# Keys and queries of rotary attention's first pair, made in the last period of the eight-bit pipeline

## The chip, the cores and the metric

The kernel runs on one core of one Trainium2 chip. The metric is the device time of one execution in microseconds (us), and the time of a kernel is the median over its runs. The engines are TensorE (PE; its weight loads are listed as PEld), VectorE (DVE), ScalarE (ACT), GpSimd (POOL) and SyncE (SP, which issues the DMAs). Each works through its own queue of instructions in order and waits on semaphores for the others.

## The reference, cut to what matters

The reference is a stack of four gated layers, each an attention-like block and a feed-forward block on `x` of shape 32 x 64 x 256 in float32, with a second input `ctx_2048` of the same shape:

```python
x = x + tanh(g_xattn[2]) * _L2_xattn_ref(_layernorm(x), ctx, mask, ...)   # block 4
x = x + tanh(g_ffn[2])   * _L2_ffn_ref(_layernorm(x), ...)                # block 5
x = x + tanh(g_xattn[3]) * _L3_xattn_ref(_layernorm(x), ctx, ...)         # block 6
x = x + tanh(g_ffn[3])   * _L3_ffn_ref(_layernorm(x), ...)                # block 7
```

Block 4 is cross attention whose query and output projections round their input and weights to eight bits, with one scale per row (`round(x / s)`, where `s = max|x| / 127`). Block 5 is a gated feed-forward network, `bit_linear(silu(bit_linear(x)) * bit_linear(x))`, which rounds each input in the same way and uses ternary weights. Block 6 is attention with rotary positions. There the 64 rows of a sequence are channels (8 heads of 8) and the 256 columns are positions:

```python
q = _apply_rotary(q_emb, split_heads(_proj(x, Wq, bq)))
k = _apply_rotary(k_emb, split_heads(_proj(c, Wk, bk)))
v = split_heads(_proj(c, Wv, bv))
scores = einsum('bhtc,bhsc->bhts', q, k) / sqrt(8)
out = einsum('bhts,bhsc->bhtc', softmax(scores), v)
```

## The kernel before

`x` stays in SBUF as 16 tiles (`NT`) of 128 rows by 256 columns. Since a sequence has 64 rows, a tile is two sequences, a pair. Blocks run one after another, and neighbours overlap.

**Blocks 4 and 5** run together in `blocks45`, a software pipeline that is written out by hand. `PERIOD` (L930) is a list of small operations, each with the number of tiles that it lags behind:

```python
xn:0 pk:0 hq5:5 r5:3 exp:2 t50:3 pv51:4 v50:4 gbo:0 vb50:4 qT:1 pat1:2 pat0:2 am:0 s50:3 pg51:4 sx:0 v51:4 aT1:2 g51:4
```

This is its first line. In period n an operation `name:back` works on tile n - back. Lags 0 to 2 belong to block 4 and lags 2 to 5 to block 5 (names with a 5). The periods run from n = 0 to 20. In period 17 block 4 works on its last tile and in period 18 its pools are closed. Every engine runs its instructions in just the order in which these operations emit them: the whole part is under a manual schedule.

The operations that the steps below name, by engine and by their lines in the profile:

- DVE: `xn` (layer norm of the next tile, L167), `xn5` (the same for block 5, L167 too), `hq5`, `xq`, `xq5` and `oq` (scaled for rounding, all L1003), `e0` and `e1` (scores plus mask, L1146), `g50` and `g51` (gate halves, L1349), `y` (L1260), `bn5` and `ag5` (statistics of block 5, L1272 and L1277), `am5h` (largest hidden value of each row, shown with all such maxima as L987).
- POOL: `sub` (scores minus their maximum, L1172), `xy` (x plus y, L1264), `gob5` (L1305), `gbo` (L1045), `vb50` and `vb51` (value half plus bias, L1358), `gv51` and `gv50` (gate half times value half, L1362).
- ACT: `exp` (L1176), `v50` and `v51` (L1354), `silu5` (L1380, with a table load before it).
- PE: products of the projections, among them `pg5` and `pv5` (L1343), and transposes (L1009).
- `w0` and `w1` (DVE and POOL): one part each of layer-norm statistics for a coming group of four tiles (`stats`, L1023). A group has eight parts: a `bn_stats` and `bn_aggr` for each tile (L110, L113), then `ln_nv` on POOL (L124) with a first guess of the inverse root on DVE (L92), then three Newton steps of four POOL operations each (L100 to L103). The last group that block 4 needs is made in periods 1 to 4. From period 5 on `w0` and `w1` emit nothing.

Block 4 uses, among others, the PSUM bank `pc` (pool `pm4`), the score tiles `e` and the tile `aT` in pool `t4`, and the places `wk` (its key weights) and `mask` in the tile `wb` of its weights.

**Block 6** (`block6`, L1445) begins with period 18. Its first `next` sets up: `gbo`, three `clear` rounds of memsets for `mx` and `va` on POOL, the statistics of tiles 0 to 3 with `_stats` on DVE (L110 to L124, L92 to L98), and `start(0)`. `start(i)` makes keys, values and queries of pair i. It takes `xn` (L167), eight products for the keys from `ctx` and eight for the queries from `xn` (L1506), the values (L1520), two rotations of two operations each on DVE (L1513), and on POOL the sum for the keys `k` (L1528), their two copies `kb` masked by head parity (L1531) and the sum for the queries `q` (L1534). Then come 140 steps g, each with score products `pp` (L1573) and the DVE reduction to `mx` (L1579), and six steps later the shifted scores `pw` (L1563) and their exponential (L1565). While periods 18 to 20 of block 5 are still being emitted, one step g is emitted at every sixth operation.

`ctx` in the layout that block 6 reads is loaded over the old one by SP at the start of period 17.

Of the kernel before, what the change touches and what calls it, by code (L numbers as in the profile page):

```python
# [17 lines left out]
F32 = mybir.dt.float32  # L18
# [4 lines left out]
ALU = mybir.AluOpType  # L23
# [3 lines left out]
P = 128  # L27
# [100 lines left out]
def _stats(c, pool, i0=0, n=NT, bufs=1, here=False):  # L128

    mv = pool.tile([P, max(n, 4), 2], F32, tag="ln_mv", name="ln_mv", bufs=bufs)[:, :n]  # L130
    for j in range(n):
        _mean(c, pool, mv[:, j, :], i0 + j, here)
    return mv, _inverse(c, pool, mv, "ln", bufs), i0


def _stats_slowly(c, pool, i0, n, bufs, on=None):

    mv = pool.tile([P, n, 2], F32, tag="ln_mv", name="ln_mv", bufs=bufs)
    for j in range(n):
        _mean(c, pool, mv[:, j, :], i0 + j)  # L140
        yield None
    yield from (None if r is None else (mv, r, i0) for r in _inverse_slowly(c, pool, mv, "ln", bufs, on))
# [20 lines left out]
def _norm(c, pool, ln, i, bufs=4):  # L163
    mv, rs, i0 = ln
    j = i - i0
    xn = pool.tile([P, D], F32, tag="xn", name="xn", bufs=bufs)
    c.nc.vector.tensor_scalar(xn, c.x[:, i, :], mv[:, j, 0:1], rs[:, j : j + 1], ALU.subtract, ALU.mult)  # L167
    return xn
# [770 lines left out]
def blocks45(c, kw):  # L939
# [26 lines left out]
    with ExitStack() as es:  # L966
# [53 lines left out]

        def stats(a):  # L1023
            if not more and a.i and len(lns) < NT // 4:
                more.append(_stats_slowly(c, sm4, 4 * len(lns), 4, 2, nc.gpsimd))
            if more and (ln := next(more[0])):
                lns.append(ln)
                more.clear()
# [326 lines left out]

        def biased(a, n):
            cols = slice(n * 512, (n + 1) * 512)
            nc.gpsimd.tensor_tensor(a.v[:, cols], a.v[:, cols], vb[:, cols], ALU.add)  # L1358

        def times(a, n):  # L1360
            cols = slice(n * 512, (n + 1) * 512)
            nc.gpsimd.tensor_tensor(a.g[:, cols], a.g[:, cols], a.v[:, cols], ALU.mult)  # L1362

        def hturned(a, n):
            a.ph[n] = turned(ps5, "ps", "ph", a.hq, 4, 4 * n)
# [44 lines left out]
        def x5(a):  # L1410
            _add_gated(c, a.i, a.po5, a.co)

        period = [(name, int(back)) for name, back in (t.split(":") for t in PERIOD.split())]
        last4 = max(back for name, back in period if name not in fifth)
        tiles = [SimpleNamespace(i=i, pat=None) for i in range(NT)]
# [14 lines left out]
        gwo = sm5.tile([P, 1], F32, tag="gwo", name="gwo")  # L1430
        nc.vector.tensor_scalar(gob, ob, c.gate[:, 6:7], None, ALU.mult)
        nc.vector.tensor_tensor(gwo, gw[:, 2:3], c.gate[:, 6:7], ALU.mult)
        for n in range(NT + max(back for _, back in period)):
            if n == NT + last4:
                es4.close()
            for name, back in period:
                if 0 <= n - back < NT and (back or n):
                    ops[name](tiles[n - back])
                    yield n - NT, n >= NT + last4

# [4 lines left out]
def block6(c):  # L1445
# [17 lines left out]
    with ExitStack() as es:  # L1463
# [16 lines left out]
        nc.vector.tensor_tensor(gbo, pb, _v(c.l3x, L3X, "bo"), ALU.add)  # L1480
        nc.vector.tensor_tensor(gbo, gbo, c.gate[:, 3:4], ALU.mult)
        mxs, vas = [], []
        for n in range(3):
            if n < 2:
                mx = sm.tile([P, 2, 4, 32], F32, tag=f"mx{n}", name=f"mx{n}")
                nc.gpsimd.memset(mx.rearrange("p t j r -> p (t j r)"), 0.0)
                mxs.append(mx)
            va = sm.tile([P, 2, 2, HN, 32], F32, tag=f"va{n}", name=f"va{n}")
            nc.gpsimd.memset(va.rearrange("p n k h r -> p (n k h r)"), 0.0)
            nc.gpsimd.memset(va.rearrange("p n k h r -> p (n k h) r")[:, :, HC], 1.0)  # L1490
            vas.append(va)

        def start(i):


            xn = _norm(c, tp, lns[i // 4], i, bufs=2)
            ctx = c.ctx.rearrange("p k t -> p (k t)")[:, i * D : (i + 1) * D]
            yield

            def project(w, src):  # L1500

                pp = pair("pp")
                for r in range(2):
                    for m in range(2):
                        rows = slice(m * S, (m + 1) * S)
                        nc.tensor.matmul(pp[:, m, r, :], w[rows, r, :], src[rows, :], start=True, stop=True)  # L1506
                return pp

            def rotate(pp, n):

                t = [tp.tile([P, 2, D], F32, tag=f"t{r}", name=f"t{r}") for r in range(2)]
                for r, f in enumerate((cos, sin)):
                    nc.vector.scalar_tensor_tensor(t[r], pp[:, :, r, :], bias[:, n, r : r + 1], f, ALU.add, ALU.mult)  # L1513
                return t

            a = [SimpleNamespace(i=i, n=n, e={}, mx=mxs[n]) for n in range(2)]
            pk = project(wk, ctx)
            pv = pair("pv").rearrange("p a b d -> p (a b d)")[:, : 2 * P].rearrange("p (j o) -> p j o", j=2)
            for j in range(2):
                nc.tensor.matmul(pv[:, j, :], ctx[:, j * P : (j + 1) * P], wv, start=True, stop=True)  # L1520
            pq = project(wq, xn)
            va = vas[i % 3]
            for n in range(2):
                src = pv[:, :, n * S : (n + 1) * S].rearrange("p k (h d) -> p k h d", d=HC)
                nc.scalar.copy(va[:, n, :, :, :HC], src)
            t = rotate(pk, 1)
            k = tp.tile([P, 2, D], F32, tag="k", name="k", bufs=1)
            nc.gpsimd.tensor_tensor(k, t[0], t[1], ALU.add)  # L1528
            kb = tp.tile([P, 2, 2, D], F32, tag="kb", name="kb", bufs=3)
            for h in range(2):  # L1530
                nc.gpsimd.tensor_scalar(kb[:, :, h, :], k, odd[:, h : h + 1], None, ALU.mult)  # L1531
            t = rotate(pq, 0)
            q = tp.tile([P, 2, D], F32, tag="q", name="q", bufs=3)
            nc.gpsimd.tensor_tensor(q, t[0], t[1], ALU.add)  # L1534
            o = tp.tile([P, 2, 2, S], F32, tag="o", name="o")
            for n in range(2):
                a[n].q, a[n].k, a[n].v, a[n].o = q[:, n], kb[:, n], va[:, n], o
            yield a
# [4 lines left out]
        def shift(a):  # L1543

            pt = ps1.tile([P, D], F32, tag="a", name="pt")
            for t in range(2):
                nc.tensor.transpose(pt[:, t * P : (t + 1) * P], a.mx[:, t].rearrange("p j r -> p (j r)"), c.ident)
            yield
            a.qs = tp.tile([P, D], F32, tag="qs", name="qs")
            nc.vector.tensor_tensor(a.qs, pt, a.q, ALU.add)  # L1550

        def scores(w, p, g, parts):
# [23 lines left out]
            for part in parts:  # L1576
                next(part, None)
            if p:
                nc.vector.tensor_reduce(p.mx[:, t, i0 : i0 + 2, 16:18], pp, AX.X, ALU.max, negate=True)  # L1579

        def mix(a, h):

# [35 lines left out]

        lns, more = [_stats(c, sm, 0, 4, bufs=2)], None
        seqs = list(start(0))[-1]
        yield
        steps, ahead = [[] for _ in range(4 * B + 13)], [[] for _ in range(4 * B + 13)]

# [375 lines left out]
```

## Time and profile before

| | |
|---|---|
| runs | 1333.27, 1330.69, 1333.59 us; median 1333.27 |
| profiled execution | 1334.85 us, of which the span is 1333.1 |
| mean granted TensorE clock | 0.97 |
| PE, DVE, ACT, POOL busy | 90%, 68%, 46%, 34% of the span |
| period of blocks 4 and 5 (starts of `sub`) | 605.53, 616.79, 629.30, 645.12, 657.64, 670.16 |
| first `mx` of block 6 | 812.93 |

In the lines of a timeline, the columns are the start in us after the span's start, the duration in us (of all that are joined under an xN), the engine, the line of the kernel, the operation, its output and inputs, and the shape. The bracket at the end is how long the engine stood idle before it, with what ended that wait. PEclk is the clock that PE was granted, in tenths of full speed in the page and as a fraction in the windows. A line of a window gives the stretch and its length, then for PE, PEld, DVE, ACT and POOL the busy us with the number of instructions, then the clock and the DMA's share and rate.

### The profile page before, as it was taken

How to read it: one execution, taken by the hardware profiler on the slowest of the kernel's cores; microseconds unless marked ns; L12 is line 12 of the kernel's file. 1: busy time of each engine (PE TensorE's matmuls, PEld its weight loads, DVE VectorE, ACT ScalarE, POOL GpSimd, SP SyncE). 2: the span in 40 equal slices, each digit the busy share in tenths (PEclk: the TensorE clock that was granted, in tenths of full speed). 3: DMA queues.
4: the chain of work that ended last, by engine and by line, in shares of the span. 5: the costliest groups of instructions: out<-in, count | busy, mean ns of one | idle time of the engine just before them, and what ended most of it. 6: DMA issues, size and time to landing. Idle time of an engine off the chain costs nothing.

```text
span 1333.1 us, 21452 instructions
## 1 busy us (share of the span) xinstructions
PE 1199.2 (90%) x8342; PEld 724.3 (54%) x8342; DVE 905.1 (68%) x2195; ACT 618.0 (46%) x1046; POOL 456.1 (34%) x479
## 2 busy tenths in 40 slices
PE   0788899999999989988899976899999999999999
PEld 0666345454533367765666642455555555555665
DVE  6588867554348898768999996587787877532111
ACT  2553634322231145657899971455555555511100
POOL 3333606120123233335777775123225335000000
PEclk9899999989999999989999997799999999999999
DMA  6000000100052120000000010100000000000000
GB/s 216 21 1 16 0 0 1 63 1 0 8 213 97 33 103 1 1 0 2 2 2 2 2 64 1 60 37 1 2 2 1 2 2 1 1 8 8 16 16 16
DMA packets 10294, 34.14 MB, mean 26 GB/s; under 512 B 1360, under 2 KB 5968, under 8 KB 8528
## 3 DMA queue, kind: packets, MB, share of 16 engines
q1 hardware_dynamic: 10192, 32.76, 6.9%
q8 instruction: 66, 1.08, 0.4%
q14 instruction: 36, 0.29, 0.1%
HBM read 30.66 MB, written 2.10 MB: 25 GB/s over the span
## 4 chain that ended last, share of the span: by engine, by line
PE 56%; DVE 28%; POOL 5%; ACT 4%; issue 4%; DMA 2%; SPq 0%; DVEq 0%; POOLq 0%; ACTq 0%
PE pw L1563 6%; PE po L1586 5%; PE pp L1573 4%; PE po L1735 4%; PE pu L1725 4%; PE pg L1725 4%; PE pc L610 3%; PE pu L462 2%; PE pg L462 2%; PE pu L465 2%; PE pa L509 2%; PE po L515 2%; PE pg L465 2%; DVE xn L167 2%; DMA w<-in_l2f 1%
## 5 line engine op out<-in xcount | busy, mean ns | idle before, releaser
L1579 DVE TENSOR_REDUCE mx<-pp 128x4 f32<-128x1024 f32 x128 | 155.9, 1218 | 42.3 <-PE pp L1573 41.8
L1565 ACT ACTIVATE e<-pw 128x1024 f32<-128x1024 f32 x128 | 130.9, 1025 | 115.0 <-PE pw L1563 68.5
L1563 PE MATMUL pw<-qs,kb 32*128 32x256 f32 x1024 | 147.1, 408 | 7.5 <-DVE qs L1550 4.5
L1573 PE MATMUL pp<-kb,q 32*128 32x512 f32 x512 | 148.8, 665 | 4.8 <-POOL q L1534 4.0
L1563 PEld LDWEIGHTS pw<-qs,kb 32*128 32x128 f32 x1024 | 88.5, 187 | 52.3 <-issue 29.4
L468 ACT ACTIVATE sg<-pg 128x512 f32<-128x512 f32 (+1 forms) x75 | 37.8, 512 | 117.1 <-PE pg L462 51.6
L610 PE MATMUL pc<-xw,wb 64*64 64x512 f32 x768 | 90.0, 600 | 0.2 <-DVE x L542 0.2
L1728 DVE TENSOR_TENSOR h<-pu,sg 128x512 f32<-128x512 f32 x32 | 22.1, 692 | 80.8 <-PE pu L1725 80.8
L1727 ACT ACTIVATE sg<-pg 128x512 f32<-128x512 f32 x32 | 19.1, 597 | 122.8 <-PE pg L1725 122.7
L469 DVE TENSOR_TENSOR h<-pu,sg 128x512 f32<-128x512 f32 (+1 forms) x75 | 42.5, 573 | 49.1 <-PE pu L462 30.4
L1528 POOL TENSOR_TENSOR k<-t,t 128x512 f32<-128x512 f32 x16 | 20.3, 1268 | 148.4 <-DVE t L1513 148.4
L1586 PE MATMUL po<-e,va 128*32 128x256 f32 x1024 | 69.0, 387 | 1.8 <-ACT e L1565 1.8
L768 POOL TENSOR_TENSOR acc<-acc,sq 128x512 f32<-128x512 f32 x28 | 39.0, 1392 | 65.1 <-ACT sq L767 63.6
L1725 PE MATMUL pg<-xf,wa 128*128 128x512 f32 x128 | 60.3, 592 | 0.0
L1725 PE MATMUL pu<-xf,wa 128*128 128x512 f32 x128 | 60.3, 592 | 0.0
L610 PEld LDWEIGHTS pc<-xw,wb 64*64 64x64 f32 x768 | 29.9, 134 | 53.9 <-issue 53.2
L1735 PE MATMUL po<-hb,h 128*128 128x256 f32 x256 | 55.9, 379 | 0.0
L1735 PEld LDWEIGHTS po<-hb,h 128*128 128x128 f32 x256 | 48.6, 190 | 8.3 <-issue 1.9
L110 DVE BATCH_NORM_STATS2 ln_st<-x 128x6 f32<-128x256 f32 x112 | 44.1, 408 | 10.9 <-POOL x L1615 7.2
L1586 PEld LDWEIGHTS po<-e,va 128*32 128x32 f32 x1024 | 26.9, 109 | 44.3 <-issue 17.5
L1513 DVE SCALAR_TENSOR_TENSOR t<-pp,wb,con 128x512 f32<-128x512 f32 x64 | 45.0, 745 | 8.7 <-PE pp L1506 8.7
L1531 POOL TENSOR_SCALAR kb<-k,con 128x512 f32<-128x512 f32 x32 | 49.8, 1569 | 1.6
(342 smaller groups left out, 2946.8 us busy)
## 6 DMA issues: line engine op xcount, KB each, us to landing
w<-in_l2f SPq DMA_DIRECT2D x12, 512.0 KB, 3.9
wa<-in_l0f SPq DMA_DIRECT2D x2, 1828.0 KB, 13.0
wa<-in_l1f SPq DMA_DIRECT2D x2, 1536.0 KB, 9.4
wa<-in_l3f SPq DMA_DIRECT2D x2, 1536.0 KB, 8.0
wb<-in_conv SPq DMA_DIRECT2D x1, 2048.0 KB, 7.4
ctx<-in_ctxT SPq DMA_DIRECT2D x2, 1024.0 KB, 6.0
ctx<-in_ctxN SPq DMA_DIRECT2D x2, 1024.0 KB, 6.3
out<-x SPq DMA_DIRECT2D x16, 128.0 KB, 1.7
```

The lines of the kernel that those rows point to most:

```text
L462: nc.tensor.matmul(p, wt[:, k, fc], xf[:, k, :N], start=k == 0, stop=False, skip_group_check=True)
L465: nc.tensor.matmul(p, wt[:, fc], z[m, s][:, :N], start=False, stop=s == 1, skip_group_check=True)
L610: nc.tensor.matmul(pcs[h][to], w[rows, k, m, h, :], xw[rows, k, h, :, Z - m : Z - m + 32], start=m == 0, stop=m == Z)
L1513: nc.vector.scalar_tensor_tensor(t[r], pp[:, :, r, :], bias[:, n, r : r + 1], f, ALU.add, ALU.mult)
L1531: nc.gpsimd.tensor_scalar(kb[:, :, h, :], k, odd[:, h : h + 1], None, ALU.mult)
L1563: nc.tensor.matmul(pw[:, jj, k, :], w.k[rows, h, k * P : (k + 1) * P], w.qs[rows, :], start=True, stop=True)
L1565: nc.scalar.activation(e, pw, AF.Exp, scale=scale)
L1573: nc.tensor.matmul(pp[:, jj], p.q[rows, t * P : (t + 1) * P], p.k[rows], start=True, stop=True)
L1579: nc.vector.tensor_reduce(p.mx[:, t, i0 : i0 + 2, 16:18], pp, AX.X, ALU.max, negate=True)
L1586: nc.tensor.matmul(po[strip(j), :], a.v[:, k, 2 * j + h, :], a.e[h, j][:, k, :], start=k == 0, stop=k == 1)
L1725: nc.tensor.matmul(p, wt[:, k, fc], xf[:, k, :], start=k == 0, stop=k == 1)
L1735: nc.tensor.matmul(po, h[:, f, q * P : (q + 1) * P], c.w2h[:, f, :], start=f == 0, stop=f == NH - 1)
```

## The change

Four things are done.

1. The statistics of tiles 0 to 3 for block 6 are made in `w0` and `w1` for tiles 10 and on, so in periods 10 to 13: two tiles' `bn_stats` and `bn_aggr` in each of periods 10 and 11, `ln_nv`, the guess and the first Newton step in 12, two Newton steps in 13. `_stats` in block 6's setup goes.
2. In period 17, at fixed counts of operations, six steps make the first pair's keys and queries: `first_features` (before the 14th operation), `first_keys` (20th), `rotated_keys` (26th), `first_queries` (32nd), `rotated_queries` (38th) and `parted_keys` (44th). Their products go to the bank `pc`, their rotated halves to an `e` tile, the summed keys to an `aT` tile, the queries to the place `wk` and the masked keys to the place `mask`. `start(0)` then makes only the values.
3. In periods 18 and 19 `vb5` and `gv5` of tiles 14 and 15 run on DVE instead of POOL: eight operations.
4. Block 6 clears `mx0` and `va0` before `start(0)`, and the rest after it.

The diff, cut to its core:

```diff
@@ -1020,7 +1020,12 @@
+        first6 = _stats_slowly(c, c.keep, 0, 4, 1, nc.gpsimd)
         def stats(a):
+            if a.i > 9:
+                c.ln6 = next(first6, None) or c.ln6
             if not more and a.i and len(lns) < NT // 4:
                 more.append(_stats_slowly(c, sm4, 4 * len(lns), 4, 2, nc.gpsimd))
             if more and (ln := next(more[0])):
@@ -1355,11 +1360,11 @@
         def biased(a, n):
             cols = slice(n * 512, (n + 1) * 512)
-            nc.gpsimd.tensor_tensor(a.v[:, cols], a.v[:, cols], vb[:, cols], ALU.add)
+            (nc.vector if a.late else nc.gpsimd).tensor_tensor(a.v[:, cols], a.v[:, cols], vb[:, cols], ALU.add)
         def times(a, n):
             cols = slice(n * 512, (n + 1) * 512)
-            nc.gpsimd.tensor_tensor(a.g[:, cols], a.g[:, cols], a.v[:, cols], ALU.mult)
+            (nc.vector if a.late else nc.gpsimd).tensor_tensor(a.g[:, cols], a.g[:, cols], a.v[:, cols], ALU.mult)
         def hturned(a, n):
             a.ph[n] = turned(ps5, "ps", "ph", a.hq, 4, 4 * n)
@@ -1410,6 +1415,56 @@
         def x5(a):
             _add_gated(c, a.i, a.po5, a.co)
+        kb6 = _v(c.wb, L2X, "mask").rearrange("p (n h d) -> p n h d", n=2, h=2)
+        q6 = _v(c.wb, L2X, "wk").rearrange("p (n d) -> p n d", n=2)
+        odd = _v(c.con, CON, "odd")
+        a6 = SimpleNamespace()
+        def products6(w, src):
+            pp = pm4.tile([P, 2, 512], F32, tag="pc", name="pp6").rearrange("p m (r d) -> p m r d", r=2)
+            w = _v(c.l3x, L3X, w).rearrange("p (r o) -> p r o", r=2)
+            for r in range(2):
+                for m in range(2):
+                    rows = slice(m * S, (m + 1) * S)
+                    nc.tensor.matmul(pp[:, m, r, :], w[rows, r, :], src[rows, :], start=True, stop=True)
+            return pp
+        def rotated6(pp, n):
+            bias = _v(c.l3x, L3X, "bias").rearrange("p (n r) -> p n r", n=2)
+            t = t4.tile([P, 4, 4, S], F32, tag="e", name="t6", bufs=3).rearrange("p j a l -> p (j a l)")
+            t = t.rearrange("p (r m d) -> p r m d", r=2, m=2)
+            for r, f in enumerate(("cos", "sin")):
+                f = _v(c.con, CON, f).unsqueeze(1).to_broadcast([P, 2, D])
+                nc.vector.scalar_tensor_tensor(t[:, r], pp[:, :, r, :], bias[:, n, r : r + 1], f, ALU.add, ALU.mult)
+            return t
+        def first_features():
+            a6.xn = _norm(c, t4, c.ln6, 0, bufs=2)
+        def first_keys():
+            a6.pk = products6("wk", c.ctx.rearrange("p k t -> p (k t)")[:, :D])
+        def rotated_keys():
+            a6.t = rotated6(a6.pk, 1)
+            a6.k = t4.tile([P, 8, P], F32, tag="aT", name="k6").rearrange("p a b -> p (a b)")[:, : 2 * D].rearrange("p (n d) -> p n d", n=2)
+            nc.gpsimd.tensor_tensor(a6.k, a6.t[:, 0], a6.t[:, 1], ALU.add)
+        def first_queries():
+            a6.pq = products6("wq", a6.xn)
+        def rotated_queries():
+            a6.t = rotated6(a6.pq, 0)
+            nc.gpsimd.tensor_tensor(q6, a6.t[:, 0], a6.t[:, 1], ALU.add)
+        def parted_keys():
+            for h in range(2):
+                nc.gpsimd.tensor_scalar(kb6[:, :, h, :], a6.k, odd[:, h : h + 1], None, ALU.mult)
+            c.first6 = kb6, q6
+        steps6 = {14: first_features, 20: first_keys, 26: rotated_keys, 32: first_queries, 38: rotated_queries, 44: parted_keys}
+        c.ln6 = None
         period = [(name, int(back)) for name, back in (t.split(":") for t in PERIOD.split())]
         last4 = max(back for name, back in period if name not in fifth)
         tiles = [SimpleNamespace(i=i, pat=None) for i in range(NT)]
@@ -1430,11 +1485,17 @@
         gwo = sm5.tile([P, 1], F32, tag="gwo", name="gwo")
         nc.vector.tensor_scalar(gob, ob, c.gate[:, 6:7], None, ALU.mult)
         nc.vector.tensor_tensor(gwo, gw[:, 2:3], c.gate[:, 6:7], ALU.mult)
+        past = 0
         for n in range(NT + max(back for _, back in period)):
             if n == NT + last4:
                 es4.close()
             for name, back in period:
                 if 0 <= n - back < NT and (back or n):
+                    if n == NT + 1:
+                        past += 1
+                        if past in steps6:
+                            steps6[past]()
+                    tiles[n - back].late = n >= NT + last4
                     ops[name](tiles[n - back])
                     yield n - NT, n >= NT + last4
@@ -1480,7 +1541,8 @@
         nc.vector.tensor_tensor(gbo, pb, _v(c.l3x, L3X, "bo"), ALU.add)
         nc.vector.tensor_tensor(gbo, gbo, c.gate[:, 3:4], ALU.mult)
         mxs, vas = [], []
-        for n in range(3):
+        def clear(n):
             if n < 2:
                 mx = sm.tile([P, 2, 4, 32], F32, tag=f"mx{n}", name=f"mx{n}")
                 nc.gpsimd.memset(mx.rearrange("p t j r -> p (t j r)"), 0.0)
@@ -1490,10 +1552,12 @@
             nc.gpsimd.memset(va.rearrange("p n k h r -> p (n k h) r")[:, :, HC], 1.0)
             vas.append(va)
+        clear(0)
         def start(i):
-            xn = _norm(c, tp, lns[i // 4], i, bufs=2)
+            xn = _norm(c, tp, lns[i // 4], i, bufs=2) if i else None
             ctx = c.ctx.rearrange("p k t -> p (k t)")[:, i * D : (i + 1) * D]
             yield
@@ -1513,25 +1577,28 @@
                     nc.vector.scalar_tensor_tensor(t[r], pp[:, :, r, :], bias[:, n, r : r + 1], f, ALU.add, ALU.mult)
                 return t
-            a = [SimpleNamespace(i=i, n=n, e={}, mx=mxs[n]) for n in range(2)]
-            pk = project(wk, ctx)
+            a = [SimpleNamespace(i=i, n=n, e={}) for n in range(2)]
+            pk = project(wk, ctx) if i else None
             pv = pair("pv").rearrange("p a b d -> p (a b d)")[:, : 2 * P].rearrange("p (j o) -> p j o", j=2)
             for j in range(2):
                 nc.tensor.matmul(pv[:, j, :], ctx[:, j * P : (j + 1) * P], wv, start=True, stop=True)
-            pq = project(wq, xn)
+            pq = project(wq, xn) if i else None
             va = vas[i % 3]
             for n in range(2):
                 src = pv[:, :, n * S : (n + 1) * S].rearrange("p k (h d) -> p k h d", d=HC)
                 nc.scalar.copy(va[:, n, :, :, :HC], src)
-            t = rotate(pk, 1)
-            k = tp.tile([P, 2, D], F32, tag="k", name="k", bufs=1)
-            nc.gpsimd.tensor_tensor(k, t[0], t[1], ALU.add)
-            kb = tp.tile([P, 2, 2, D], F32, tag="kb", name="kb", bufs=3)
-            for h in range(2):
-                nc.gpsimd.tensor_scalar(kb[:, :, h, :], k, odd[:, h : h + 1], None, ALU.mult)
-            t = rotate(pq, 0)
-            q = tp.tile([P, 2, D], F32, tag="q", name="q", bufs=3)
-            nc.gpsimd.tensor_tensor(q, t[0], t[1], ALU.add)
+            if i:
+                t = rotate(pk, 1)
+                k = tp.tile([P, 2, D], F32, tag="k", name="k", bufs=1)
+                nc.gpsimd.tensor_tensor(k, t[0], t[1], ALU.add)
+                kb = tp.tile([P, 2, 2, D], F32, tag="kb", name="kb", bufs=3)
+                for h in range(2):
+                    nc.gpsimd.tensor_scalar(kb[:, :, h, :], k, odd[:, h : h + 1], None, ALU.mult)
+                t = rotate(pq, 0)
+                q = tp.tile([P, 2, D], F32, tag="q", name="q", bufs=3)
+                nc.gpsimd.tensor_tensor(q, t[0], t[1], ALU.add)
+            else:
+                kb, q = c.first6
             o = tp.tile([P, 2, 2, S], F32, tag="o", name="o")
             for n in range(2):
                 a[n].q, a[n].k, a[n].v, a[n].o = q[:, n], kb[:, n], va[:, n], o
@@ -1544,7 +1611,7 @@
             pt = ps1.tile([P, D], F32, tag="a", name="pt")
             for t in range(2):
-                nc.tensor.transpose(pt[:, t * P : (t + 1) * P], a.mx[:, t].rearrange("p j r -> p (j r)"), c.ident)
+                nc.tensor.transpose(pt[:, t * P : (t + 1) * P], mxs[a.n][:, t].rearrange("p j r -> p (j r)"), c.ident)
             yield
             a.qs = tp.tile([P, D], F32, tag="qs", name="qs")
             nc.vector.tensor_tensor(a.qs, pt, a.q, ALU.add)
@@ -1576,7 +1643,7 @@
             for part in parts:
                 next(part, None)
             if p:
-                nc.vector.tensor_reduce(p.mx[:, t, i0 : i0 + 2, 16:18], pp, AX.X, ALU.max, negate=True)
+                nc.vector.tensor_reduce(mxs[p.n][:, t, i0 : i0 + 2, 16:18], pp, AX.X, ALU.max, negate=True)
         def mix(a, h):
@@ -1618,8 +1685,10 @@
-        lns, more = [_stats(c, sm, 0, 4, bufs=2)], None
+        lns, more = [c.ln6], None
         seqs = list(start(0))[-1]
+        clear(1)
+        clear(2)
         yield
         steps, ahead = [[] for _ in range(4 * B + 13)], [[] for _ in range(4 * B + 13)]
```

## The prediction, made before the changed kernel was timed

> **What bounds the kernel now.** I read the page first (busy tenths and granted clock by slices), then the windows by stage, then the timelines of VectorE (DVE) and GpSimd (POOL) of two periods of the eight-bit pipeline, and last the timeline of the seam where rotary attention starts. Measurement of this kernel can tell about 0.2%, some 2.7 us, from no change; so sizes of 1 us decide here.
>
> Page, 40 slices of 33.3 us: slices 20 to 24 are the stretch where the eight-bit blocks run alone, 25 and 26 are the seam and what follows.
>
> ```profile
> PE   0788899999999989988899976899999999999999
> DVE  6588867554348898768999996587787877532111
> POOL 3333606120123233335777775123225335000000
> PEclk9899999989999999989999997799999999999999
> ```
>
> TensorE (PE) has its worst digits (7, 6) and clock (7, 7) at the seam. By windows:
>
> ```profile
> core 0: us, PE busy (x) PEld busy (x) DVE busy (x) ACT busy (x) POOL busy (x), PEclk, DMA share, GB/s
> 646.00:796.00 150.00, 136.39 (x1601) 94.51 (x1599) 145.86 (x470) 141.04 (x248) 112.32 (x95) 0.99 0.04 16
> 796.00:811.00 15.00, 5.74 (x28) 3.43 (x28) 10.22 (x36) 1.71 (x4) 10.79 (x15) 0.84 0.00 1
> 811.00:866.00 55.00, 43.50 (x260) 22.96 (x260) 31.89 (x53) 19.86 (x27) 17.97 (x15) 0.76 0.09 32
> ```
>
> From 646 to 796 DVE is busy 145.86 of 150 us: it sets the period of 12.52 us (POOL's first subtraction, L1172, starts at 645.12, 657.64, 670.16). What is put on DVE there lengthens the period. In the seam, 796 to 811, no engine is full: it is a chain.
>
> The steady period, POOL then DVE:
>
> ```profile
> 650.34 2.50 POOL L1358 TENSOR_TENSOR v<-v,wb 128x512 f32<-128x512 f32 x2
> 653.45 2.50 POOL L1362 TENSOR_TENSOR g<-g,v 128x512 f32<-128x512 f32 x2 [0.61 <-ACT g L1380]
> ...
> 652.89 0.41 DVE L167 TENSOR_SCALAR xn<-x,mv,l_s 128x256 f32<-128x256 f32 x1
> 653.22 0.34 DVE L1003 TENSOR_SCALAR xq<-xn,sr 128x256 f32<-128x256 f32 x1
> ```
>
> Block 5's xn5 (L167) and block 4's xq (L1003) lie between the end of POOL's vb5 (652.84) and the start of its gv5 (653.45). One period earlier they do not:
>
> ```profile
> 635.79 2.50 POOL L1358 TENSOR_TENSOR v<-v,wb 128x512 f32<-128x512 f32 x2
> 638.38 2.55 POOL L1362 TENSOR_TENSOR g<-g,v 128x512 f32<-128x512 f32 x2
> ...
> 632.96 0.43 DVE L1272 BATCH_NORM_STATS2 ln_st<-x 128x6 f32<-128x256 f32 x1 [1.31 <-POOL x L1264]
> ...
> 638.35 1.45 DVE L167 TENSOR_SCALAR xn<-x,mv,l_s 128x256 f32<-128x256 f32 x1
> 639.72 1.35 DVE L1003 TENSOR_SCALAR xq<-xn,sr 128x256 f32<-128x256 f32 x1
> ```
>
> There two Newton steps of a group's statistics, eight POOL operations (L100 to L103), stood ahead of x (L1264). bn5 waited 1.31 us, gv5 followed vb5 without a gap, and xn5 and xq took 1.45 and 1.35 instead of 0.41 and 0.34: a DVE tensor-by-scalar from SBUF to SBUF is held while a POOL operation runs. That period, 629.30 to 645.12, was 15.82 long, 3.30 over the steady one.
>
> The seam:
>
> ```profile
> 804.96 1.27 POOL L1528 TENSOR_TENSOR k<-t,t 128x512 f32<-128x512 f32 x1 [3.94 <-DVE t L1513]
> 806.33 3.12 POOL L1531 TENSOR_SCALAR kb<-k,con 128x512 f32<-128x512 f32 x2
> 809.41 1.26 POOL L1534 TENSOR_TENSOR q<-t,t 128x512 f32<-128x512 f32 x1
> ...
> 803.70 2.08 PE L1506 MATMUL pp<-xn,wb 64*128 64x256 f32 x8 [5.28 <-DVE xn L167]
> ...
> 810.73 2.07 PE L1573 MATMUL pp<-kb,q 32*128 32x512 f32 x4 [3.98 <-POOL q L1534]
> ...
> 812.93 1.22 DVE L1579 TENSOR_REDUCE mx<-pp 128x4 f32<-128x1024 f32 x1 [5.08 <-PE pp L1573]
> ```
>
> From the hq5 of period 18 (DVE L1003, 797.19) the chain runs statistics (798.71 to 803.1), xn, query products, rotation, POOL's k, kb, q, first score products, first maximum at 812.93: 15.74 us, with 9.26 us of PE idle.
>
> **The change part by part.** Each part is priced against this profiled execution (1334.85 us, span 1333.1). That is 1.6 us above the median of the runs (1333.27); the sum is a difference and is put on the median.
>
> *Statistics moved into periods 10 to 13.* They leave 4.4 us of the seam's chain. In periods 10 and 11 DVE gets two bn_stats and two aggregates each: at 593.39 and 593.95 such pairs follow each other by 0.53, so 1.06; bn5 has about 0.13 of wait to absorb it (g ends 647.79, bn5 starts 647.98): 0.9. That moves xn of the next tile (648.73), with it POOL's gbo (649.21) and vb5, whose end goes from 652.84 to 653.75. ScalarE (ACT) does not move: its silu (L1380) starts 652.25 behind a table load and ends 653.31. So gv5 follows vb5 with no gap, as at 638.38, and xq surely, xn5 nearly surely, meets it. Price from the rows: 1.01 for xq, 1.04 for xn5; I take 1.7, between the one and both. Two periods: 2 x (0.9 + 1.7) = 5.2. Bounds: 1.8 if neither is held, 5.9 if both are.
> Here the Trainium skill speaks against me: "SBUF — State Buffer", section "Who interferes with whom", says that the instruction that starts first gets the shared ports for its whole length, and the other blocks. By it an xn5 started just ahead of gv5 wins and only POOL is delayed, 2 x 0.9 = 1.8. The row says otherwise: xn5 is shown starting at 638.35, gv5 at 638.38, and xn5 was held for 1.04. The row decides; the rule sets the low end.
> Period 12: the guess (DVE, L92) waits for ln_nv on POOL behind the subtraction. In the trace (619.01) that wait was 1.67 with DVE otherwise idle and the period still 12.51; y ends 0.1 after the subtraction in the steady period, so 0.2. Queued behind it on DVE is g (L1349). Period 13: two Newton steps, eight POOL operations ahead of x and gob5, as at 629.30: 3.3. Sum of this part before the seam: 5.2 + 0.2 + 3.3 = 8.7.
>
> *Keys and queries of the first pair in period 17.* PE does the same 16 products there (two of 1.13, beside slack of 1.7 to 1.8 in that period): nothing; without that slack 2.3. The DMA of ctx is issued as before (779.98, about 6 us to land), before the keys need it. DVE gets xn 0.41 and two rotations of 1.40: 3.2. POOL gets k 1.27, q 1.26, kb 3.12 = 5.65, against 0.91 + 2.38 of idle there. k waits for DVE's rotation with the second vb5 behind it; q sits ahead of half a gv5, for which amh (793.77) waits, and kb ahead of x (795.44), for which bn5 waits. Following the queues: second gv5 ends about 798.0 instead of 793.06, amh to 799.3, kb ends about 801.1, x 801.8, bn5 801.9, hq 802.2 instead of 797.19: 5.0 later. After it there are no statistics, no products, no rotation: the score products need kb6 and q6, both there at 801.1, and PE's pb, pv and pm, so they run about 803 to 805.1 at the slow 2.08; but the first mx now stands on DVE behind the first late vb5, which waits for ACT's v (L1354, 0.70) of a pm (1.04) behind the score products. That puts it at about 808.2. Gain 812.93 - 808.2 = 4.7; bounds 7.5 (mx at 805.4, straight after the products) and 2.
>
> *Late vb5 and gv5 on DVE.* Eight operations of 1.25 to 1.3 leave POOL; the nearest DVE rows are 0.68 (L1146, one operand in PSUM) and 0.86 (L529). 8 x 0.8 = 6.4 us, in a stretch where DVE is busy 31.89 of 55: hidden, beyond the wait counted above. Without that cover, 6.4; with POOL's k, kb, q no longer behind vb5, a gain of up to 2. I take 0.
>
> *Clears 1 and 2 after the start:* POOL memsets, 0.95 each, with POOL idle 3.94 after them before: nothing; if the va copy waited, 1.
>
> *The clock.* The seam's products run at half speed: 2.08 for eight L1506 products at 803.70, 1.14 at 824.34. The skill's "TensorE: Matmul & The Clock Gate", Part 1, says the clock falls after an idle window of about 3.4 us. By it, the end of PE's idle 5.28 and 3.98 would bring back up to 1 us on each of three products, 3 in all. But PE's products at 838.70 and 855.02 still take 1.22 where others take 0.70, with no idle over 2.63 near them; the same sparse mix follows after the change. I take 0, and 3 as the end.
>
> Sum: 8.7 - 4.7 = 4.0 slower, 1333.3 + 4.0 = 1337.3.
>
> **The rivals.**
> 1. *Faster.* DVE's xn5 and xq get through before gv5 (rule above), so periods 10 and 11 cost 1.8; the seam gains its 7.5. 1.8 + 0.2 + 3.3 - 7.5 = -2.2, with part of the clock's 3 about -4: 1329.3. For it: a margin of hundredths at 638.35. Against it: vb5's end moves 0.9 and the gap was 0.61. It decides where xn5 starts more than about 0.1 before gv5.
> 2. *Same.* No collision but the seam as priced: 5.3 - 4.7 = +0.6, 1333.9.
> 3. *Slower still.* The seam gives back only 1 to 2, because hq, bn5 and the late vb5 wait for one another behind POOL's 5.65: 8.7 - 1.5 = +7.2, 1340.5.
> That it does not do what it says is little likely: the first 16 products stand ahead of block 4's end in each engine's order, and the old ones are gone.
>
> **How the numbers follow.** The sum 0.47, rival 3 0.16, rival 2 0.17, rival 1 0.20. The sum's own range, 1335.5 to 1339.5, with its bounds (5.9 instead of 5.2, clock) stays above the 0.2%. Slower is 0.47 + 0.16 = 0.63, same 0.17, faster 0.20. The range takes in rival 1's centre and most of rival 3: 1329.5 to 1341.
>
> **What would show it.** Periods 10 and 11 of about 15.1 between subtractions, with xq at 1.3 and xn5 over 0.41; period 13 near 15.8; period 17 starting 8 to 9 us late; first mx 3 to 5 us later than 812.93 in absolute time (816 to 818); after 866 + 4 the same spacing. I am wrong if periods 10 and 11 stay under 13.6, or if the first mx comes before 812.

## The result, and the profile after

The changed kernel takes 1339.17 us in the median of five runs (1336.58 to 1339.88), against 1331.05 for the kernel before in the same set. The ratio is 1.0061, with a 95% interval from 1.0047 to 1.0076: 8.1 us slower (6.3 to 10.1). The prediction was 4.0 slower (1337.3), in a range from 1329.5 to 1341, which is from 3.8 faster to 7.7 slower counted from 1333.27. The direction was right and the size half: the time itself lies inside the range, the difference of 8.1 just beyond its end.

The profiled execution of the changed kernel took 1336.58, its fastest; that of before had taken 1334.85, slower than its median. So their spans (1334.8 and 1333.1) differ by only 1.7. The two also differ before the change can act: `sub` of the fifth period starts at 645.12 before and at 642.53 after. I therefore compare stretches between marks, not absolute times: from the `sub` of period 9 to that of period 16, from there to the first `mx`, and from the first `mx` to the last.

The page of the changed kernel, same 40 slices:

```profile
PE   0789899999999999987898787799999999999999
DVE  6588777645359898758999997687787877532111
POOL 3332606210113233326676666023225335000000
PEclk9899999999999999979999996899999999999999
```

PE's digits are lower in slices 22 and 23 (8 and 7, about 700 to 767 us), where they were 9 and 9 before: those are periods 10 to 13. In slices 24 and 25 (767 to 834), with the seam, they are 8 and 7 where they were 7 and 6, and in slice 26 it is 7 where it was 8. In a period with two `bn_stats` (period 10), first POOL, then DVE:

```profile
710.96 2.51 POOL L1363 TENSOR_TENSOR v<-v,wb 128x512 f32<-128x512 f32 x2
713.55 2.56 POOL L1367 TENSOR_TENSOR g<-g,v 128x512 f32<-128x512 f32 x2
720.31 1.90 POOL L1177 TENSOR_TENSOR e<-e,m 128x1024 f32<-128x1024 f32 x1 [4.21 <-DVE m L1173]
...
713.51 1.47 DVE L167 TENSOR_SCALAR xn<-x,mv,l_s 128x256 f32<-128x256 f32 x1
714.90 1.36 DVE L1003 TENSOR_SCALAR xq<-xn,sr 128x256 f32<-128x256 f32 x1
```

gv5 (L1367) follows vb5 (L1363) without a gap, xn5 takes 1.47 and xq 1.36: the picture that the prediction took from 638.35. It is so in four periods, not in three. The starts of `sub` are 705.05, 720.31, 735.54, 750.75 and 766.57, which makes 15.26, 15.23, 15.21 and 15.82. From period 9 to 16 the pipeline loses 11.4 us. Period 12 is the one that I had priced at 0.2. Its POOL and DVE:

```profile
737.53 0.19 POOL L124 TENSOR_SCALAR ln_nv<-ln_mv 128x4 f32<-128x4 f32 x1
737.80 0.73 POOL L1269 TENSOR_TENSOR x<-x,y 128x256 f32<-128x256 f32 x1
738.49 0.20 POOL L100 TENSOR_TENSOR ln_t<-ln_r 128x4 f32<-128x4 f32 x1
738.76 0.20 POOL L101 TENSOR_TENSOR ln_t<-ln_t,ln_nv 128x4 f32<-128x4 f32 x1
739.05 0.22 POOL L102 TENSOR_SCALAR ln_t<-ln_t 128x4 f32<-128x4 f32 x1
739.36 0.20 POOL L103 TENSOR_TENSOR ln_r<-ln_r,ln_t 128x4 f32<-128x4 f32 x1
739.51 0.79 POOL L1310 TENSOR_TENSOR x<-x,gob 128x256 f32<-128x256 f32 x1
740.26 1.17 POOL L1050 TENSOR_TENSOR x<-x,gbo 128x256 f32<-128x256 f32 x1
741.40 2.52 POOL L1363 TENSOR_TENSOR v<-v,wb 128x512 f32<-128x512 f32 x2
743.99 2.55 POOL L1367 TENSOR_TENSOR g<-g,v 128x512 f32<-128x512 f32 x2
...
737.75 0.17 DVE L92 TENSOR_SCALAR ln_r<-ln_nv 128x4 int32<-128x4 int32 x1 [0.20 <-POOL ln_nv L124]
...
739.63 1.22 DVE L1003 TENSOR_SCALAR hq<-g,shr 128x1024 f32<-128x1024 f32 x1
...
743.95 1.47 DVE L167 TENSOR_SCALAR xn<-x,mv,l_s 128x256 f32<-128x256 f32 x1
745.34 1.36 DVE L1003 TENSOR_SCALAR xq<-xn,sr 128x256 f32<-128x256 f32 x1
```

The wait of the guess is 0.20, as priced. But the Newton step behind it, 738.49 to 739.56 with its gaps, stands ahead of gob5, gbo and vb5. They have no idle time left between them, and vb5 ends at 743.92, so gv5 follows it at once and meets xn5. DVE comes late as well: hq5 takes 1.22 beside gob5 where it took 0.75 in period 10 (709.66), and with the 0.20 of the guess xn5 stands 8.41 behind `sub`, against 7.77 in the steady period.

The seam of the changed kernel:

```profile
807.14 3.23 POOL L1463 TENSOR_SCALAR wb<-k,con 128x512 f32<-128x512 f32 x2
810.34 0.72 POOL L1269 TENSOR_TENSOR x<-x,y 128x256 f32<-128x256 f32 x1
...
811.09 0.43 DVE L1277 BATCH_NORM_STATS2 ln_st<-x 128x6 f32<-128x256 f32 x1 [1.57 <-POOL x L1269]
...
811.84 1.59 DVE L1003 TENSOR_SCALAR hq<-g,shr 128x1024 f32<-128x1024 f32 x1
...
813.98 0.69 DVE L1363 TENSOR_TENSOR v<-v,wb 128x512 f32<-128x512 f32 x1
...
814.71 1.21 DVE L1646 TENSOR_REDUCE mx<-pp 128x4 f32<-128x1024 f32 x1
```

As predicted, bn5 waits for x (`xy`) behind the masked keys, hq5 comes 5.9 us later in its period (797.19 before, 811.84 now: 14.65 later, of which 8.77 is the lag of the last `sub`), and the late vb5 stands ahead of the first `mx`. That comes 2.87 after hq5's start, where it was 15.74. From the last `sub` to the first `mx` it is 23.13, before 30.12: 7.0 gained, where I had 4.7.

### The profile page after: what moved, and what is told of

It reads as the page before. It is cut to its first block, busy times and chain, and to the rows that moved or that the text cites. A ratio compares the mean times of both kernels' runs of the same rounds, so it can differ in the third digit from the quotient of the medians.

```text
span 1334.8 us, 21433 instructions
## 1 busy us (share of the span) xinstructions
PE 1198.8 (90%) x8326; PEld 725.2 (54%) x8342; DVE 918.4 (69%) x2193; ACT 617.9 (46%) x1046; POOL 448.4 (34%) x484
## 4 chain that ended last, share of the span: by engine, by line
PE 57%; DVE 28%; POOL 5%; ACT 4%; issue 4%; DMA 2%; SPq 0%; POOLq 0%; DVEq 0%; ACTq 0%
PE pw L1630 6%; PE po L1653 5%; PE pp L1640 4%; PE po L1804 4%; PE pu L1794 4%; PE pg L1794 4%; PE pc L610 3%; PE pu L462 2%; PE pg L462 2%; PE pu L465 2%; DVE xn L167 2%; PE pa L509 2%; PE po L515 2%; PE pg L465 2%; PE pp L1570 1%
## 5 line engine op out<-in xcount | busy, mean ns | idle before, releaser
L1630 PE MATMUL pw<-qs,kb 32*128 32x256 f32 x960 | 134.5, 400 | 5.2 <-DVE qs L1617 4.3
L1640 PE MATMUL pp<-kb,q 32*128 32x512 f32 x480 | 136.2, 642 | 0.3 <-ACT e L1632 0.3
L1630 PEld LDWEIGHTS pw<-qs,kb 32*128 32x128 f32 x960 | 81.3, 184 | 46.8 <-issue 28.7
L1348 PE MATMUL pm<-w,xqT 128*128 128x512 bf16 x112 | 38.6, 422 | 11.8 <-DVE sh L992 7.6
L1177 POOL TENSOR_TENSOR e<-e,m 128x1024 f32<-128x1024 f32 x16 | 30.4, 1902 | 55.0 <-DVE m L1173 39.0
```

What stands on the lines that cost most here:

```text
L1630: nc.tensor.matmul(pw[:, jj, k, :], w.k[rows, h, k * P : (k + 1) * P], w.qs[rows, :], start=True, stop=True)
L1640: nc.tensor.matmul(pp[:, jj], p.q[rows, t * P : (t + 1) * P], p.k[rows], start=True, stop=True)
```

## The experiments

Each was timed in rounds against the kernel before, on one chip for a set. Two theories stood at the start. Theory A: the statistics cost more in the pipeline than in the seam, because they close the gap between vb5 and gv5. Theory B: the statistics are cheap, and the loss is made in period 17 and behind it. The marks of all profiles, as differences to the profile of before:

| kernel | sub 9 to 16 | to first mx | first to last mx | ratio of the runs, 95% |
|---|---|---|---|---|
| the change | +11.4 | -7.0 | -0.1 | 1.0061 (1.0047 to 1.0076) |
| the change again | +11.4 | -7.0 | -0.2 | 1.0054 (1.0041 to 1.0066) |
| statistics only | +11.5 | -3.7 | -0.9 | 1.0064 (1.0051 to 1.0077) |
| no statistics | -0.1 | -7.0 | +1.4 | 0.9962 (0.9950 to 0.9974) |
| statistics behind xq | +8.9 | -7.0 | +2.2 | 1.0027 (1.0015 to 1.0040) |
| vb5, gv5 back on POOL | +11.4 | -7.5 | -2.9 | 1.0039 (1.0028 to 1.0051) |
| statistics in gaps | +2.3 | -7.0 | +2.6 | 0.9996 (0.9986 to 1.0005) |
| that, keys at the end | +2.3 | -4.2 | +2.9 | 1.0017 (1.0009 to 1.0024) |
| gaps, vb5, gv5 on POOL | +2.3 | -7.5 | -1.7 | 0.9967 (0.9956 to 0.9978) |
| vb5, gv5 on DVE only | -0.1 | +0.2 | +3.5 | 1.0029 (1.0018 to 1.0039) |
| gaps, POOL, queries later | +2.3 | -6.8 | -2.7 | 0.9962 (0.9949 to 0.9975) |

The columns are the stretches between the marks named above, in us; the first column of the profile of before is 87.63, the second 30.12, the third 331.91. Up to the first `mx` kernels with the same work repeat to about 0.1. The two profiles of the change agree in the third column too (-0.1 and -0.2), but kernels with the same work behind the first `mx` differ there (no statistics +1.4, statistics in gaps +2.6). Behind the last `mx` all twelve profiles take 188.2 within 0.1.

**The change again**, as a control, with no edit.

> The changed kernel once more, as the control of this set. Both theories: about 8 us slower than before (ratio 1.006), and in its profile the four periods of 15.26, 15.23, 15.21 and 15.82 between the starts of sub that the first profile shows. If the net of its profile (lag of the pipeline less the gain of the seam) is again near 4 while the medians differ by 8, the rest lies in the clock's windows and not in the order of the work.

Measured: 1337.45 against 1330.66, and the same four periods (15.24, 15.25, 15.20, 15.82). The net of its marks is 4.2 and that of the runs 6.8. The kernels differ from execution to execution ahead of the marks and between the first and the last `mx`; single profiles don't place the remainder.

**Statistics only.** The kernel before, and in it:

```diff
+        first6 = _stats_slowly(c, c.keep, 0, 4, 1, nc.gpsimd)
         def stats(a):
+            if a.i > 9:
+                c.ln6 = next(first6, None) or c.ln6
...
-        lns, more = [_stats(c, sm, 0, 4, bufs=2)], None
+        lns, more = [c.ln6], None
```

> Only the statistics are moved into periods 10 to 13; keys, queries, vb5, gv5 and the clears stay as before. Theory A (the statistics cost more in the pipeline than they cost in the seam, because they push gv5 against vb5 so that xn5 and xq are held): the periods grow by 2.7, 2.7, 2.7 and 3.3, 11.4 in all, the seam loses 4.4: 7 slower, ratio 1.005. Theory B (the statistics are cheap where they are put and the loss is made in period 17 and behind it): 4.4 less with 2 to 3 of added DVE work, so 2 faster, 0.9985.

Measured: 1338.08, 7.4 slower; periods of 15.26, 15.25, 15.21 and 15.81; the seam gains 3.7. Theory A holds, and theory B's claim that the statistics are cheap falls: this part alone is as slow as the whole change.

**No statistics.**

```diff
-            if a.i > 9:
-                c.ln6 = next(first6, None) or c.ln6
...
-        c.ln6 = None
+        c.ln6 = (mv6, r6, 0)     # two small tiles, set once to 0 and 1
```

> The change without the statistics of tiles 0 to 3 of block 6: a mean of 0 and an inverse deviation of 1 take their place, so this part of the computation is left out. The rest is as changed. Theory A: the 11.4 us of the pipeline go, so 3.3 (from the median's 8.1) to 7 (from the seam in the profile) faster than before, ratio 0.995 to 0.9975. Theory B: still 4 or more slower than before.

Measured: 1325.32, 5.3 faster than before; all periods 12.50 to 12.51. Against the change in the same set (1337.45) the statistics cost 12.1; the marks up to period 16 say 11.5. Theory A again.

**Statistics behind xq.**

```diff
-        first6 = _stats_slowly(c, c.keep, 0, 4, 1, nc.gpsimd)
+        first6 = _stats_slowly(c, c.keep, 0, 4, 1)
...
             a.xq = raised(t4, "xq", a.xn, a.sr, D)
+            if a.i > 9:
+                for _ in range(2):
+                    c.ln6 = next(first6, None) or c.ln6
```

> The change with all eight parts of the statistics put directly behind xq in DVE's order, two in each of periods 10 to 13, and the Newton steps on DVE instead of POOL. The same values, about 4.3 us of DVE work (2 x 1.06 and about 2.2 for the small operations). Theory A: nothing is pushed between xn and gv5, so xn5 and xq stay at 0.41 and 0.34, and each of the four periods grows by about 1.1 only: 7 less than the change, so between 3 faster and 1 slower than before. Theory B: as slow as the change, ratio 1.006.

Measured: 1334.22, 3.6 slower than before, so better than the change by 3.2, outside the expected range (3 faster to 1 slower than before). The periods tell why: 13.56, 13.56, 15.34 and 16.48. In the first two, xn5 (0.41) and xq (0.35) are free and the price is 1.05 each, just the work. In the third, DVE and POOL:

```profile
727.17 0.41 DVE L167 TENSOR_SCALAR xn<-x,mv,l_s 128x256 f32<-128x256 f32 x1
727.50 0.35 DVE L1003 TENSOR_SCALAR xq<-xn,sr 128x256 f32<-128x256 f32 x1
727.77 0.16 DVE L124 TENSOR_SCALAR ln_nv<-ln_mv 128x4 f32<-128x4 f32 x1
727.96 1.12 DVE L92 TENSOR_SCALAR ln_r<-ln_nv 128x4 int32<-128x4 int32 x1
729.12 1.18 DVE L96 TENSOR_TENSOR ln_t<-ln_r 128x4 f32<-128x4 f32 x1
...
727.73 2.56 POOL L1368 TENSOR_TENSOR g<-g,v 128x512 f32<-128x512 f32 x2 [0.59 <-ACT g L1386]
```

The guess (4 elements wide, 0.17 elsewhere) takes 1.12 and the square of r, which reads SBUF twice, 1.18: they lie beside gv5's two halves, and each ends within 0.1 of the end of its half. In the fourth period two products of a Newton step are held likewise (1.27 at 743.89 and 1.19 at 745.20), and DVE waits 0.69 for PE. So the hold reaches instructions that I had thought too small to matter. Not all of them: ln_nv, which reads every second element, takes 0.16 although gv5 has begun; which property decides was not tested. That an operation with two SBUF inputs contends with a GpSimd one that reads SBUF is stated by the Trainium skill, "SBUF — State Buffer", section "Who interferes with whom", and the row of 729.12 agrees.

**Statistics in the gaps.** A generator of the same values, advanced at three places:

```diff
             a.xq = raised(t4, "xq", a.xn, a.sr, D)
+            if a.i in (10, 11):          # two bn_stats, bn_aggr each
+                next(first6)
+                next(first6)
...
             a.xq5 = raised(t5, "xq", a.xn5, a.sr5, D)
+            if a.i == 9:                 # ln_nv and guess, DVE
+                next(first6)
...
             # behind gv50
+            if n == 0 and a.i in (9, 10, 11):   # one Newton step, POOL
+                next(first6)
```

> The change with the statistics put where neither engine pushes the other: two bn_stats and aggregates behind xq in periods 10 and 11 (1.05 each, as in the kernel with all behind xq), ln_nv and the guess on DVE behind xq5 in period 12 (0.4), and one Newton step on POOL behind the last gv5 of periods 13, 14 and 15, where POOL idles 1.68 us and a step takes 1.15. Theory A (shared ports): no operation of 0.34 to 0.41 becomes one of 1.3, only oq and xq5 may be held by 0.2 each: 2.1 + 0.4 + 0.6 at most over the kernel without statistics, so about 2.3 faster than before, ratio 0.998. If any POOL work in the period costs DVE its own length, 3.5 more: 1 slower.

Measured: 1330.27 against 1329.95, ratio 0.9996: no difference to before, where 2.3 faster was expected. The periods are 13.55, 13.55, 12.78 and then 12.50 to 12.51. A Newton step on POOL between gv5 and `sub`:

```profile
740.95 2.51 POOL L1387 TENSOR_TENSOR g<-g,v 128x512 f32<-128x512 f32 x2 [0.59 <-ACT g L1407]
743.42 0.25 POOL L1033 TENSOR_TENSOR ln_t<-ln_r 128x4 f32<-128x4 f32 x1
743.75 0.20 POOL L1034 TENSOR_TENSOR ln_t<-ln_t,ln_nv 128x4 f32<-128x4 f32 x1
744.03 0.22 POOL L1035 TENSOR_SCALAR ln_t<-ln_t 128x4 f32<-128x4 f32 x1
744.34 0.20 POOL L1036 TENSOR_TENSOR ln_r<-ln_r,ln_t 128x4 f32<-128x4 f32 x1
745.14 1.90 POOL L1195 TENSOR_TENSOR e<-e,m 128x1024 f32<-128x1024 f32 x1 [0.61 <-DVE m L1191]
```

`sub` still waits for DVE's m, by 0.61, and the period is 12.5: the step costs nothing there, where period 12 grew by 2.7 with it ahead of gob5. By the marks up to period 16 the statistics went from 11.4 to 2.3, so the periods came as expected. By the runs they went from 12.1 to about 4.5 (0.9996 less 0.9962 of 1330, not in one set): what is missing lies elsewhere, in part behind the first `mx`, where this profile loses 2.6 and that without statistics 1.4.

**vb5 and gv5 back on POOL**, in the change as it is:

```diff
-                    tiles[n - back].late = n >= NT + last4
+                    tiles[n - back].late = False
```

> The change with vb5 and gv5 of tiles 14 and 15 left on POOL, as before. If DVE's slack behind the seam hides the eight operations, and POOL's too, the time is that of the change within 1.5 us (ratio to before 1.0045 to 1.0065), since the seam's first mx only loses its 0.7 behind the late vb5. If the move matters (POOL's k, kb and q of pair 1 stand behind vb5 when it is left on POOL), it is 2 to 4 us slower than the change, 1.0075 or more.

Measured: 1335.85 against 1329.95, ratio 1.0039 (1.0028 to 1.0051) where the change has 1.0054 and 1.0061: 2 to 3 us better, though the intervals overlap. The second theory expected it 2 to 4 slower, since POOL would not be relieved: it falls. **On DVE only**, the same move put into the kernel before:

```diff
-            nc.gpsimd.tensor_tensor(a.v[:, cols], a.v[:, cols], vb[:, cols], ALU.add)
+            (nc.vector if a.late else nc.gpsimd).tensor_tensor(...)
...
+                    tiles[n - back].late = n >= NT + last4
```

> The kernel before with only vb5 and gv5 of tiles 14 and 15 put on DVE. If they cost because mx stands behind them: 2 to 3 slower than before, ratio 1.0015 to 1.0025. If DVE's slack hides them (my prediction), 1.000; if POOL's relief brings the second pair's k, kb and q forward, up to 2 faster, 0.9985.

Measured: 1335.02 against 1330.18, ratio 1.0029 (2.4 to 5.2 us slower): the move is not free. The marks place it between the first `mx` and the last: +3.5. One wait in this kernel is easy to see: at 846.50 gv5 has waited 1.54 for ACT's silu, and the ninth `mx` stands behind it on DVE. But the loss is not made there. Counted from the first `mx`, the fifth is already 4.3 later than in the kernel before (20.47 against 16.13), the eighth 3.3, the ninth 4.8, and the tenth again 3.2: the wait comes and is made good. Up to the fifth `mx`, first the kernel before and then this one:

```profile
824.34 1.14 PE L1506 MATMUL pp<-xn,wb 64*128 64x256 f32 x8 [0.58 <-ACT va L1525]
827.11 0.35 DVE L1003 TENSOR_SCALAR xq<-xn,sr 128x256 f32<-128x256 f32 x1
827.89 1.13 PE L1573 MATMUL pp<-kb,q 32*128 32x512 f32 x4
...
824.02 2.08 PE L1507 MATMUL pp<-xn,wb 64*128 64x256 f32 x8 [0.58 <-ACT va L1526]
827.61 0.68 DVE L1362 TENSOR_TENSOR g<-g,v 128x512 f32<-128x512 f32 x1
828.20 1.35 DVE L1003 TENSOR_SCALAR xq<-xn,sr 128x256 f32<-128x256 f32 x1
830.23 2.08 PE L1574 MATMUL pp<-kb,q 32*128 32x512 f32 x4
```

A gv5 stands ahead of xq5 on DVE, xq5 is held by 1.0 beside POOL's q (828.05), and both products on PE take 2.08 instead of 1.13 and 1.14. From 12 to 24 us behind the first `mx` the granted clock is 0.50 here and 0.88 in the kernel before. It is 0.82 to 0.88 in the four profiles with vb5 and gv5 on POOL (before; back on POOL; gaps, vb5, gv5 on POOL; queries later), and 0.50 to 0.64 in the eight with them on DVE. So the move's cost is in part DVE's order and in part PE's clock, which comes back later. How much each is worth, and why the clock follows the move, no run here separates.

**Both repairs: the statistics in the gaps, and vb5 and gv5 on POOL.** The two edits above together.

> The statistics in the gaps, the first keys and queries in period 17 as changed, and vb5 and gv5 of tiles 14 and 15 left on POOL. If the move to DVE costs what the two profiles say (the eight operations stand ahead of mx in DVE's order and one waits 1.54 us for ACT's silu; 851.98 against 849.12 at the tenth mx, 3.2 after alignment by the first), this is 2 to 3 faster than with the statistics in the gaps alone, ratio to before 0.9975 to 0.9985. If the move is free, 0.9996 as that one.

Measured: 1325.69 against 1330.18, ratio 0.9967 (0.9956 to 0.9978): 4.4 faster than before, some 12 faster than the change. This beats both kernels. Against the statistics in the gaps alone it is 3.9 better (0.9996 less 0.9967), more than the 2 to 3 expected, and as much as the move cost in the kernel before. (The expectation's 3.2 at the tenth `mx` is 2.0 by its own records: 37.27 less 35.28 from the first.)

**Keys at the end** of period 17, on the kernel with the statistics in the gaps:

```diff
-        steps6 = {14: first_features, ..., 38: rotated_queries, 44: parted_keys}
+        steps6 = {14: first_features, ..., 38: rotated_queries, 60: parted_keys}   # with q's sum on POOL too
```

> The kernel with the statistics in the gaps, and of period 17's steps the queries' sum (POOL 1.26) and the masked keys (3.12) put behind x, as the last POOL work before gob5, instead of ahead of a half of gv5 and of x. If hq5 of period 18 was late because bn5 waits for POOL's x behind those (5.9 us in the profile of the change), it comes 3 to 4 earlier, the first score products wait for the keys instead, and the first mx comes about 0.8 earlier: 0.5 to 2 better than with the statistics in the gaps alone. If the score products' wait for the keys is the bound, no difference.

Measured: ratio 1.0017, 2.8 slower than with them at 44. My expectation was wrong. hq5 of period 18 came 2 us earlier after the last `sub`, but the first score products then waited for the keys, on PE:

```profile
805.60 1.82 PE L1662 MATMUL pp<-wb 32*128 32x512 f32 x4 [2.89 <-POOL wb L1485]
```

PE is idle for 2.89, and the first `mx` comes 2.8 later from the last `sub` (25.91 against 23.12). **Queries behind xq5**, on the kernel with both repairs:

```diff
-        steps6 = {..., 38: rotated_queries, 44: parted_keys}
+        steps6 = {..., 43: rotated_queries, 44: parted_keys}
```

> The kernel with the statistics in the gaps and vb5, gv5 on POOL, and of period 17's steps the rotation of the queries with POOL's sum put behind oq and xq5 instead of ahead of them, so that the last half of gv5 runs 1.26 earlier. If am5h's wait for that half (0.53 in the profile of the change) and the held oq and xq5 are on the path: 0.5 to 1.5 faster than without this. If the masked keys set the first score products: no difference, or 1 slower by the later sum.

Measured: 1325.50, ratio 0.9962 beside 0.9967: no difference that these runs can show. In the profile bn5 now waits 2.80 for x behind the masked keys, and the first `mx` comes 0.7 later.

## Why the prediction was right in sign and short in size

- *Statistics in periods 10 and 11: right.* 2.6 each predicted, 2.7 measured (15.26 and 15.23 less 12.52). xn5 comes 0.7 later behind `sub`, where I had 0.9; xn5 and xq both were held, 2.1 together, where I had 1.7. The row of 638.35 was the better guide than the rule that whoever starts first gets the ports (the Trainium skill, "SBUF — State Buffer", section "Who interferes with whom"): at 713.51 xn5 is again shown starting 0.04 ahead of gv5, and is held.
- *Period 12: a step that failed.* 0.2 predicted, 2.7 measured. I priced the wait of the guess and put the first Newton step, which is issued in the same period ahead of gob5, gbo and vb5 on POOL, at nothing. The period that I took as the model, 616.79 to 629.30, has the same step, and there vb5 ends at 624.71 with xn5 already held to 0.79. It cost nothing there: gv5 still began 0.40 behind vb5, so xq passed in 0.34, and DVE had 1.67 of idle time. That the same step can cost nothing elsewhere is shown by the kernel with the statistics in the gaps; it moves ln_nv and the guess as well, and the three were not moved one at a time.
- *Period 13: right.* 3.3 predicted, 15.82 less 12.52 measured.
- *The seam: right in its mechanism, too small.* 4.7 predicted to the first `mx`, 7.0 measured. The late hq5 was sized well (5.0 against 5.9). What came sooner than I had it is the rest: the products for the late vb5 ran ahead of the score products (L1348 at 810.43, L1640 at 811.42), DVE was never idle behind hq5, and the first `mx` followed it by 2.87, where I had taken 6.0.
- *vb5 and gv5 on DVE: the second step that failed.* 0 predicted, with DVE's idle time as the cover. Measured alone: 3.9 by the runs. I had priced the work and the one wait ahead of the first `mx`. I had not priced what stands behind these operations on DVE up to the fifth `mx`, nor that PE would stay at half clock there.
- *The clock: right at 0 as a sum, by luck.* The stretch from the first to the last `mx` changed by 0.1 only, but the clock did move. The first score products took 1.35 instead of 2.07 (L1640 at 811.42), to no use, since `mx` waited for DVE. The queries' products of the second pair went the other way, from 1.14 (824.34) to 2.08 (L1570 at 825.59). From 815 to 830 the granted clock was 0.54, with PE busy for 13.04 of the 15 us.

Of the signs that I had named, periods 10, 11 and 13 came as said. Period 17 was 8.8 late as said, but by coincidence: 11.4 were lost, and this profile was 2.6 ahead of the other at the first mark. For the same reason, and since the seam gained more, the first `mx` came at 814.71 and not at 816 to 818.

So the sum that the runs support is: statistics 12.1, the move to DVE 3.9, and for the rest of the seam the remainder of the change's 7.2 in that set, 8.8 gained (7.5 by the marks, with the move taken back). The failed sizes partly cancel, which is luck and the reason why 4.0 was as near as it was. Open is a remainder of about 2 us: with statistics at 2.3 by the marks, the two kernels with the statistics in the gaps should be 2.6 and 6.5 faster than before, and are 0.5 and 4.4. In the profiles it shows behind the first `mx`: +2.6 for the statistics in the gaps against -0.1 for the change, with the same work there and a granted clock of 0.67 against 0.72 in the first 40 us. And ahead of the marks the profiles differ by up to 4 us (the `sub` of period 5 lies between 641.15 and 645.12); nothing here says why.

## What to carry to other kernels

Before work is moved into a full pipeline, look at what it pushes against what: here 1 us of small work cost 2.7, because it closed a gap of 0.6 between two GpSimd operations through which two VectorE operations passed. Price every instruction that a moved step issues on each queue, not the one that waits; then try the places where the other engine stands idle. An engine's idle time is no cover: ask what is queued behind the operation that is moved there. And before a wait is called the cause, follow the marks one by one: the longest wait in sight, 1.54, was made good at the next mark, and the loss had been made four marks earlier.

## What the runs showed of the hardware

An operation on a few elements can be held as long as a large one: the guess on 128x4 took 1.12 instead of 0.17, and a product of 128x4 that reads SBUF twice 1.18 instead of 0.16, each beside one half of a GpSimd pair of 2.56. It does not catch every small operation: ln_nv on the same 128x4 took 0.16 beside the same pair. Between small GpSimd operations there was nothing of the kind: beside the Newton step, oq took 0.38 and xq5 0.34.

Moving eight operations of 128x512 from GpSimd to VectorE went along with a lower TensorE clock: 0.50 to 0.64 in the eight profiles that have the move, 0.82 to 0.88 in the four that don't, from 12 to 24 us behind the first `mx`.
